# First graph's loads ahead of the constants, and adjacency loads as transfers, in the planner of a two-layer graph attention kernel

## The chip, the cores and the metric

The kernel runs on one core of a Trainium2 chip. The metric is the device time of one execution in microseconds (us); three executions of the kernel before took 3692.64 to 3694.01 us, with a median of 3692.82. The engines are named as in the profile: PE is the matrix engine, PEld its weight loads, DVE the vector engine, ACT the scalar engine, POOL GpSimd, SP the queue engine that issues most of the transfers. The profile was taken of one execution of 3692.5 us from its first to its last instruction, with a mean granted TensorE clock of 0.996.

## The reference

There are 32 graphs of 512 nodes with 512 features each, `x[32, 512, 512]` in float32, and an adjacency matrix for each, `adj[32, 512, 512]` in int32. Cut to what matters:

```
h = relu(layernorm(x))                                    # layer 0
scores = leaky_relu(h@w_src [rows] + h@w_dst [columns] + b)
attn = softmax(where(adj + I == 0, -inf, scores), rows)
x = x + attn @ h

h = relu(layernorm(x))                                    # layer 1: two attention layers
xl = h @ W1                                               # 4 heads of 256
e = leaky_relu(xl.att_src1 [sources] + xl.att_dst1 [targets])
g = softmax(where(adj > 0 or I, e, -1e9), over sources)^T @ xl + b1, heads joined
g = elu(g)                                                # 1024 features
g2 = the same with W2, att_src2, att_dst2, b2, one head of 512
x = x + g2
```

The adjacency matrix of a graph is used twice over, as a mask with the diagonal set: by rows in layer 0 and by columns in both attention layers of layer 1. Both uses need the mask and its transpose.

## The kernel before

**Work and tiles.** A graph is four tiles of 128 nodes. x of a graph is one buffer `x` (1 MB), loaded by `load_x` (L653) through SP; the adjacency matrix is loaded by `load_adj` (L660) through GpSimd, which turns int32 into bfloat16 on the way (512 KB in the buffer), once as `m0` for layer 0 (`masks0`, L673) and once as `m1` for layer 1 (`masks1`, L689). There are two places for x, one for m0, two for m1.

**A graph's path.** `layer0_scores` (L708) takes the statistics of x (L493, L494, L495 on DVE; a power of -1/2 on GpSimd, L497; L502 on DVE), makes h on ACT (L510) and two dot products of each h tile with the score vectors `ws_r` and `wd_r` on DVE (L378), adds b (L720), and makes the mask m0: four additions of the identity to diagonal blocks (L680), one pass that turns zeros into a large negative number (L683), and four transposing transfers through SP (L669). `edge_weights` (L582) makes the attention weights: row maxima on DVE (L591, then L596 and L598), spreading by PE transposes (L487), a leaky ReLU on ACT (L609), a subtraction on DVE (L612), the mask's addition on GpSimd (L614), an exponential on ACT (L617). `layer0_out` multiplies with h on PE (L627). `layer1_in` normalises again and transposes h; `layer1_project` and `layer2_project` multiply with W1 and W2 by a scheme that needs seven products instead of eight (L822), `layer1_scores` and `layer1_head` handle the four heads, `layer2_out` the last attention and the store. `masks1` makes m1 with one pass over the whole matrix (L695) and four products on the diagonal blocks (L701).

**Constants.** `load_constants` (L388) fetches the two score vectors and b of layer 0 first (with a rank 400 places ahead), then the two attention vectors of the first attention layer (into a place of the kind `E`), eight pieces of W1, and with a rank 300 places behind, b1, b2, the second attention vectors and W2. `scores_1` and `scores_2` form dot products of the weights with the attention vectors on DVE (L378 with w as input), `sums` forms the sums of weights for the seven products (L470 on DVE or L471 on GpSimd).

**What sets the order.** The kernel writes its program by a planner. Every operation is handed to `Plan.op` with the engines that can do it, a cost, what it reads and what it writes; `Plan.draft` then plays the whole program through as a list scheduler: always the engine that can begin earliest goes next, with GpSimd asked before SP when both can begin at one time, and takes the waiting operation of lowest rank among those whose inputs are there by then. The first draft's rank is the place in the program less `ahead`; each later draft, six in all, ranks by the latest time found from the draft before. The best draft gives the order in which instructions are written to each engine's queue. On the chip each engine runs its queue in that order; the waits there come from the tiles that instructions share, not from the planner's times.

A cost is (time on the engine, time to the result), and for transfers a third number: the time for which the one transfer line is taken. Such transfers queue behind each other on that line, and at most eight of them are on their way (`IN_FLIGHT`, L51). Another 60 ns (`SIGNAL`) go by before a result is seen elsewhere. `by_dma(n)` (L255) gives 350 ns of issue, 2000 ns after, and n bytes at 300 bytes per ns. A DVE pass over n elements costs n/0.96 + 70 ns and 85 more to its result; four times as fast in the mask passes. Operations with `lock=True` on DVE and GpSimd exclude each other in the draft. The calls at the start (L968 on) are `load_x(0)`, `load_constants()`, `layer0_scores(0)`, `scores_1`, `sums`, `layer0_out(0)`, `layer1_in(0)`, then `load_x(1)` and `layer0_scores(1)`, and the loop over graphs.

The places that an edit of this kind meets in the planner are these:

```
            for held in moves:
                if len(landed) >= self.IN_FLIGHT:
                    at = max(at, landed[-self.IN_FLIGHT])
                moving = max(moving, at) + held
                there += moving - at
                landed.append(at + there)
```

The other functions, with their line numbers:

## Time and profile before

| what | value |
|---|---|
| median of three executions | 3692.82 us |
| span of the profiled execution | 3692.5 us |
| transfers of the whole span | 312.17 MB, mean 85 GB/s |
| loads of adj, `m<-in_adj_dram` | 64 of 512 KB, median 7.0 us from issue to landing |
| loads of x, `x<-in_x_dram` | 32 of 1024 KB |
| transposing transfers `m0T<-m` | 128, median 4.2 us to landing |
| chain that ended last: PE, DVE, DMA | 94%, 3%, 1% of the span |

In the profile's groups a line such as "L614 POOL TENSOR_TENSOR E<-E,m" names the source line, the engine, the operation and the tiles written and read, with the digits of their names left out: m stands for m0 and m1, w for the pieces of the weights. A timeline row gives the start, the stretch, the engine, and in square brackets how long the engine had been idle before and what ended that. Engines that end in q (SPq) are the issuing of an instruction, not its work. A table of stretches gives for each the length, then busy time with the number of instructions for PE, PEld, DVE, ACT and POOL, then the granted clock of PE, the busy share of the transfer engines and the GB/s that they moved.

### The profile page before, as it was taken

The numbers are of one execution on the slowest core, as the hardware profiler recorded it, in microseconds if no ns is written. First come the engines' busy times: TensorE is split into PE (matmuls) and PEld (weight loads), VectorE is DVE, ScalarE is ACT, GpSimd is POOL, SyncE is SP. The second block draws the span as 40 slices with busy tenths as digits, with TensorE's granted clock in tenths as the row PEclk, the third lists the DMA queues.
The fourth block names the chain that finished last, engine by engine and source line by source line (L and its number), as shares of the span: only waits on it lengthen the run. The fifth ranks groups of instructions, "written<-read, shape, count | busy, mean of one in ns | idle before, by whom it ended". The sixth has DMA issues, their size and how long they took to land.

```text
span 3692.5 us, 51317 instructions
## 1 busy us (share of the span) xinstructions
PE 3625.2 (98%) x17806; PEld 3131.3 (85%) x17806; DVE 2878.2 (78%) x7478; ACT 1760.2 (48%) x3227; POOL 1592.1 (43%) x1353
## 2 busy tenths in 40 slices
PE   5899999999999999999999999999999999999998
PEld 4788888888888888888888888888888888888887
DVE  7988778877788877788877878777887778787755
ACT  2455444554454554445544445544455544455433
POOL 3534444534444444445344444444444444444332
PEclk9999999999999999999999999999999999999999
DMA  6244322334323333223333233442233422334310
GB/s 162 52 92 103 87 73 82 81 92 104 72 74 90 75 103 91 70 83 80 91 103 72 76 88 75 103 98 68 81 82 85 103 72 78 86 75 103 90 51 32
DMA packets 304342, 312.17 MB, mean 85 GB/s; under 512 B 150496, under 2 KB 188880, under 8 KB 304080
## 3 DMA queue, kind: packets, MB, share of 16 engines
q1 hardware_dynamic: 270288, 275.32, 26.2%
q0 software_dynamic: 33792, 33.56, 6.5%
q8 instruction: 140, 2.29, 0.3%
q14 instruction: 122, 1.00, 0.1%
HBM read 240.91 MB, written 67.89 MB: 84 GB/s over the span
## 4 chain that ended last, share of the span: by engine, by line
PE 94%; DVE 3%; DMA 1%; POOL 0%; issue 0%; ACT 0%; DVEq 0%; ACTq 0%
PE acc L627 46%; PE acc L822 41%; PE acc L487 4%; PE m_bank L487 2%; DVE junk L591 1%; DVE junk L378 0%; PE acc L553 0%; DVE E L612 0%; DMA m<-in_adj_dram 0%; DVE v L905 0%; POOL E_one L614 0%; DVE E_one L612 0%; DMA x<-in_x_dram 0%; DVE v L893 0%; DMA out_dram<-x 0%
## 5 line engine op out<-in xcount | busy, mean ns | idle before, releaser
L614 POOL TENSOR_TENSOR E<-E,m 128x512 f32<-128x512 f32 x512 | 620.2, 1240 | 803.3 <-DVE E L612 798.3
L627 PE MATMUL acc<-pair,E 128*128 128x257 f32 x4096 | 961.6, 381 | 1.4 <-ACT E L617 1.2
L627 PEld LDWEIGHTS acc<-pair,E 128*128 128x128 f32 x4096 | 743.0, 190 | 114.5 <-ACT E L617 14.4
L822 PE MATMUL acc<-w_T,E 128*128 128x257 f32 (+1 forms) x2048 | 521.5, 381 | 1.0 <-ACT pair L522 0.6
L627 PE MATMUL acc<-h,E_one 128*128 128x256 f32 (+1 forms) x2048 | 478.2, 382 | 6.3 <-ACT E_one L617 6.3
L617 ACT ACTIVATE E<-E 128x512 f32<-128x512 f32 x512 | 312.0, 624 | 315.4 <-POOL E L614 315.4
L627 PE MATMUL acc<-xl,E_one 128*128 128x257 f32 x1984 | 448.2, 379 | 0.0
L591 DVE CUSTOM_DVE_ANT_0 junk<-m1T,a_bank 128x512 bf16<-128x512 bf16 x640 | 436.0, 681 | 15.4 <-PE a_bank L487 1.7
L627 PEld LDWEIGHTS acc<-h,E_one 128*128 128x128 f32 x2048 | 383.8, 191 | 59.4 <-ACT E_one L617 7.6
L822 PEld LDWEIGHTS acc<-w_T,E 128*128 128x128 f32 x2048 | 379.6, 190 | 55.4 <-ACT pair L522 0.8
L627 PEld LDWEIGHTS acc<-xl,E_one 128*128 128x128 f32 x1984 | 371.4, 190 | 53.7
L612 DVE TENSOR_TENSOR E<-E,m_bank 128x512 f32<-128x512 f32 x512 | 326.5, 679 | 24.7 <-PE m_bank L487 24.7
L609 ACT ACTIVATE E<-c_row,ac 128x512 f32<-128x512 f32 x512 | 335.6, 708 | 1.9 <-DMA c_row<-lines 1.9
L520 ACT COPY pair<-acc 128x258 f32<-128x258 f32 (+1 forms) x375 | 138.2, 369 | 412.1 <-PE acc L822 410.3
L520 ACT COPY xl<-acc 128x257 f32<-128x257 f32 x219 | 81.7, 373 | 455.8 <-PE acc L822 455.8
L902 ACT ACTIVATE e<-v,minus_one 128x512 f32<-128x512 f32 x256 | 184.3, 720 | 236.4 <-DVE r L639 111.1
L645 DVE SCALAR_TENSOR_TENSOR x<-acc,r,x 128x256 f32<-128x256 f32 x512 | 240.6, 478 | 47.8 <-PE acc L627 43.6
L663 POOL DMA_DIRECT2D m<-in_adj_dram x64 | 51.4, 804 | 521.1 <-DVE col L591 476.8
L835 DVE TENSOR_TENSOR pair<-acc,pair 128x258 f32<-128x258 f32 (+1 forms) x390 | 164.5, 424 | 137.8 <-PE acc L822 127.7
L822 PE MATMUL acc<-w,hT 128*128 128x258 f32 x1024 | 268.4, 382 | 0.0
L822 PE MATMUL acc<-w,pair 128*128 128x257 f32 x1024 | 259.3, 380 | 0.0
L614 POOL TENSOR_TENSOR E_one<-E_one,m 128x512 f32<-128x512 f32 x128 | 145.0, 1165 | 263.2 <-DVE E_one L612 263.2
(108 smaller groups left out, 6117.7 us busy)
## 6 DMA issues: line engine op xcount, KB each, us to landing
a_row<-lines SPq DMA_DIRECT2D x190, 256.0 KB, 3.4
c_row<-lines SPq DMA_DIRECT2D x190, 256.0 KB, 3.5
x<-in_x_dram SPq DMA_DIRECT2D x32, 1024.0 KB
m<-in_adj_dram POOLq DMA_DIRECT2D x64, 512.0 KB, 7.0
spill<-x SPq DMA_DIRECT2D x32, 1024.0 KB, 4.3
x<-spill SPq DMA_DIRECT2D x32, 1024.0 KB
out_dram<-x SPq DMA_DIRECT2D x30, 1024.0 KB, 5.0
m0T<-m SPq DMA_TRANSPOSE x128, 4.2
```

The lines of the kernel that those rows point to most:

```text
L487: op("PE", on_pe(P, transpose=True), lambda: nc.tensor.transpose(dst_of(), src_of(), identity), src, dst(part), ahead)
L520: nc.scalar.copy(dst_of(), src_of())
L591: lambda t=t: nc.vector.tensor_tensor_reduce(junk, mask_max.at[:, t, :], a_row.at, 1.0, LOWEST, ALU.add, ALU.max, accum_out=amax.at[:, t : ...
L609: lambda t=t: nc.scalar.activation(E.at[:, t, :], c_row.at, AF.Prelu, bias=a_of(t), scale=1.0, alpha=SLOPE),
L612: op("DVE", on_dve(N), lambda t=t: nc.vector.tensor_sub(E.at[:, t, :], E.at[:, t, :], m_row.at), m_row(*ROW) + E(t), E(t))
L614: "POOL", on_pool(N, True), lambda t=t: nc.gpsimd.tensor_add(E.at[:, t, :], E.at[:, t, :], mask.at[:, t, :]),
L617: op("ACT", on_act(N), lambda t=t: nc.scalar.activation(E.at[:, t, :], E.at[:, t, :], AF.Exp), E(t), E(t))
L627: lambda s=s: nc.tensor.matmul(acc.at[:, :n], E.at[:, s, node_block(t)], of(s), start=(s == 0), stop=(s == T - 1)),
L645: lambda acc=acc, r=r, f=f, t=t: nc.vector.scalar_tensor_tensor(X.at[:, t, f], acc.at[:, :HD], r.at, X.at[:, t, f], op0=ALU.mult, op1=ALU. ...
L822: lambda k=k: nc.tensor.matmul(acc.at[:, :width], at[a]()[:, k, node_block(r)], weight_of(w, k, c), start=(first and k == 0), stop=(k == n ...
L835: op("DVE", on_dve(width), lambda: nc.vector.tensor_add(place(), acc.at[:, :width], place()), acc(0) + token, token)
L902: op("ACT", on_act(2 * F, 1), lambda e=e, ts=ts: nc.scalar.activation(e.at, v.at[:, ts, :], AF.Exp, bias=minus_one), parts, e(0))
```

## The change

At the start, two tokens are brought in that only the planner knows: `START("x")`, written by the load of x of graph 0, and `START("adj")`, written by the first load of an adjacency matrix. All other loads of x, and all constants but the two score vectors and b of layer 0, read the first; all other adjacency loads read the second. In the draft they so begin once the load they are behind has landed. The purpose is that graph 0 has the transfer line for itself at first. Besides, an adjacency load's cost changes from 2200 ns on GpSimd and 8000 to landing, outside the transfer line, to 1100 ns on GpSimd, 4500 to landing and 2800 on the line, so it also counts among the eight transfers on their way.

```
+        behind = START("x")
         att = [Buffer("E"), Buffer("E")]
         for i, vector in enumerate((att_src1, att_dst1)):
-            fetch(HF, lambda i=i: flat(att[0])[:, i * HF : (i + 1) * HF], rows(vector, HF), att[0](i), 0)
+            fetch(HF, lambda i=i: flat(att[0])[:, i * HF : (i + 1) * HF], rows(vector, HF), att[0](i), 0, behind)
...
+    START = Buffer(None)
...
     def load_x(b):
         X[b] = xb = Buffer("x")
         op(
             "SP", by_dma(4 * N * D), lambda: nc.sync.dma_start(xb.at, node_tiles(x, b)),
-            (), xb(*((t, half) for t in range(T) for half in range(2))),
+            START("x") if b else (), xb(*((t, half) for t in range(T) for half in range(2))) + ([] if b else START("x")),
         )
...
-        op("POOL", (2200.0, 8000.0), lambda: nc.gpsimd.dma_start(m.at, node_tiles(adj, b)), (), m(*ROW))
+        first = not START.wrote.get("adj")
+        op(
+            "POOL", (1100.0, 4500.0, 2800.0), lambda: nc.gpsimd.dma_start(m.at, node_tiles(adj, b)),
+            () if first else START("adj"), m(*ROW) + (START("adj") if first else []),
+        )
```

The pieces of W1, b1, b2, the second attention vectors and W2 get `behind` in the same way as the two attention vectors shown.

More of the change, by code (lines that the diff above doesn't have):

```diff
@@ L388, in load_constants, with fetch @@
     def load_constants():
-        def fetch(n, place, src, token, ahead):
-            op("SP", by_dma(4 * P * n), lambda: nc.sync.dma_start(place(), src), (), token, ahead)
+        def fetch(n, place, src, token, ahead, behind=()):
+            op("SP", by_dma(4 * P * n), lambda: nc.sync.dma_start(place(), src), behind, token, ahead)
         fetch(D, lambda: ws_r, rows(w_src, D), W["w0"](0), AHEAD)
@@ L404, in load_constants @@
                     H // 2 * F, lambda k=k, q=q: w1_s[q][:, k % (KD // 2), :, 2:], w1_k[k, :, half::2, :],
-                    W["w1"]((q, k % (KD // 2))), 0,
+                    W["w1"]((q, k % (KD // 2))), 0, behind,
                 )
-        fetch(HF, lambda: b1_r, rows(b1, HF), W["b1"](1), -LATER)
-        fetch(D, lambda: b2_r, rows(b2, D), W["b2"](0), -LATER)
+        fetch(HF, lambda: b1_r, rows(b1, HF), W["b1"](1), -LATER, behind)
+        fetch(D, lambda: b2_r, rows(b2, D), W["b2"](0), -LATER, behind)
         for i, vector in enumerate((att_src2, att_dst2)):
-            fetch(D, lambda i=i: flat(att[1])[:, i * D : (i + 1) * D], rows(vector, D), att[1](i), -LATER)
+            fetch(D, lambda i=i: flat(att[1])[:, i * D : (i + 1) * D], rows(vector, D), att[1](i), -LATER, behind)
         nk = KH // 2
@@ L416, in load_constants @@
                     nk * HD, lambda q=q, half=half: w2_s[q] if half else w2_s[q][:, :, 2:],
-                    w2_q[i, :, :, W2 - 2 :] if half else w2_q[i, :, :, : W2 - 2], W["w2"](*((q, k) for k in range(nk))), -LATER,
+                    w2_q[i, :, :, W2 - 2 :] if half else w2_q[i, :, :, : W2 - 2], W["w2"](*((q, k) for k in range(nk))), -LATER, behind,
                 )
```

## The prediction, made before the changed kernel ran

> **What bounds the kernel now.** I read the page's busy table and its 40 slices first, then busy time by stretches of 100 us and, at the start, of 10 us, then the first 30 us of the timeline, and last the landing times of the adjacency loads. Busy table and slices:

> ```profile
> PE 3625.2 (98%) x17806; PEld 3131.3 (85%) x17806; DVE 2878.2 (78%) x7478; ACT 1760.2 (48%) x3227; POOL 1592.1 (43%) x1353
> ...
> PE   5899999999999999999999999999999999999998
> ```

> The span is 3692.5 us and PE is busy for 3625.2, so all that any edit of the order can move is 67.3 us of idle PE. By stretches of 100 us, 48.4 of it lie in 0 to 100, 6.1 in 100 to 200, 2.2 in 200 to 400, none from 400 to 3600, and 10.5 after 3600. The change starts at the start, so here are stretches of it (busy us, instructions in brackets):

> ```profile
> 0.00:10.00 10.00, 0.00 (x0) 0.00 (x0) 3.00 (x11) 1.28 (x1) 3.31 (x13) 1.00 0.74 194
> 10.00:20.00 10.00, 0.00 (x0) 0.00 (x0) 1.13 (x6) 2.93 (x4) 1.22 (x1) 1.00 1.12 299
> 20.00:30.00 10.00, 2.73 (x8) 1.48 (x8) 8.73 (x23) 0.53 (x1) 0.00 (x0) 1.00 1.22 267
> 30.00:40.00 10.00, 3.71 (x10) 2.85 (x11) 9.66 (x29) 3.78 (x7) 5.61 (x5) 1.00 0.97 307
> ...
> 50.00:60.00 10.00, 3.87 (x18) 3.03 (x17) 9.41 (x34) 0.01 (x1) 3.79 (x2) 0.96 0.00 0
> ```

> The third figure is DVE. Up to 20 us nothing computes; from 22 to about 165 us DVE is full (9.3 to 10 of 10 in most stretches) and PE has holes. So DVE sets the pace of the start: a microsecond of DVE idleness before 22 us is worth about one microsecond at the end, until PE is full. The timeline of DVE there (start, duration, and in brackets idle before and what ended it):

> ```profile
> 6.08 2.47 DVE L493 BATCH_NORM_STATS2 st<-x 128x6 f32<-128x512 f32 x4 [4.49 <-DMA x<-in_x_dram]
> 8.47 0.36 DVE L494 BATCH_NORM_AGGREGATE mv<-st 128x2 f32<-128x6 f32 x4
> 14.08 0.29 DVE L680 TENSOR_TENSOR m<-m,ident 128x128 bf16<-128x128 bf16 x1 [5.24 <-DMA m<-in_adj_dram]
> 14.29 0.16 DVE L495 TENSOR_SCALAR col<-mv 128x4 f32<-128x4 f32 x1
> 14.36 0.69 DVE L680 TENSOR_TENSOR m<-m,ident 128x128 bf16<-128x128 bf16 x3
> 15.79 0.16 DVE L502 SCALAR_TENSOR_TENSOR col<-mv,col 128x4 f32<-128x4 f32 x1 [0.74 <-POOL col L497]
> 20.80 0.69 DVE L695 TENSOR_SCALAR m<-m 128x2048 bf16<-128x2048 bf16 x1 [4.84 <-DMA m<-in_adj_dram]
> 21.41 0.69 DVE L683 TENSOR_SCALAR m<-m 128x2048 bf16<-128x2048 bf16 x1
> 22.01 0.69 DVE L378 SCALAR_TENSOR_TENSOR junk<-h,ws_r 128x512 bf16<-128x512 f32 x1
> ```

> Two stalls are to be seen. L680 needs m0 of graph 0, which lands at 14.0; behind it in DVE's order stands L495, which needed only x. Then L695 needs m1 of graph 0, which is not wanted for long, and holds L683 and all eight dots for 4.84 us. The eight dots then end with L720 at 27.97.

> [...] GpSimd issues three adjacency loads at 1.51, about 2.3 and 3.27; the times to landing are 12.5, 18.3 and 21.5 us, so they land one after another, at 14.0, 20.6 and 24.8. [...]

> **The change part by part.** START is a Buffer(None): no tile. Its tokens exist for the planner only; no instruction on the chip waits for them. What the change alters is the planner's clock, and so the order on each queue. I first replayed the old rules by hand to see whether they give the traced order. Old: x lands at 2000 + 3495 = 5.5 us; m0 at 8.0, the second adjacency load at 2200 + 8000 = 10.2. Four L493 end at 7.97, L494 at 8.28, L680 is ready at 8.06, L495 only at 8.43: one L680, then L495, then three L680, as traced. L683 and L695 become ready within some 20 ns of each other at 10.25 (L680 waits out GpSimd's lock until 9.7), and L695 went first. On SP, eight transfers in flight let seven weight loads go before the mask is there, then four transposes: also as traced. So the method carries.

> New, the same way. (a) At time 0 the planner asks GpSimd before SP, so the first adjacency load takes the transfer line first: 2800, plus 4500: it lands at 7.3. x comes behind: 2800 + 3495 + 2000 = 8.3. Four L680 run from 7.36 to 8.17, L683 is ready at 8.32, x's statistics at 8.36. So the order on DVE becomes L680 x4, L683, L493 x4, L494 x4, L495, L502, dots. (b) m1 of graph 0 is now held to 7.36 and lands at 15.3, behind the dots' start; L695 falls behind the dots. (c) On SP at 8.36: x of graph 1 and the two attention vectors (three issues of 350), then at 9.4 the transposes, ready at 9.07 and more urgent; the eight W1 pieces now come after them.

> What this does on the chip: the issues ahead on both queues stay x, two score vectors, b, x of graph 1, attention vectors on SP, and three adjacency loads on GpSimd, with no wait. [...] So m0 should land at about 14.0 again, with 13 to 15 as bounds. From there, with durations of the rows above: L680 x4 and L683, 0.95 + 0.6, to 15.6; L493 x4 and L494, 2.75, to 18.35; L495, 0.15; L497 on GpSimd 1.22 (its row), to 19.8; L502 0.16; first L510 0.85, to 20.9; eight dots at 0.74, to 26.8, against 27.97. Gain 1.1. L695 (0.6) is not saved but moves behind 27 us, where DVE is full: gain left about 0.5 to 1.1. The removed stall of 4.84 is thus mostly paid back, since 2.75 of statistics that had hidden in the wait for m0 now stand behind it, and the pow, L502 and L510 lie open again.

> Transposes: SP now waits in the first of them to 15.6 instead of issuing weights; four took 6.62, to 22.2. Eight W1 pieces of 256 KB follow, 2 MB at the 267 to 307 GB/s of the stretches, 7 to 8 us: the last lands at 30 to 31. The first dot with W1 ran at 33.70, so I cost this at nothing; its cover is the work between 27 and 34 (four L591, L493 of x, L596, L598). E_one's addition ran at 35.54 behind L612, and the transposed mask is there by 25: nothing. The constants in the diff's other lines change place on SP only: nothing, since SP waits for none of them.

> (d) All 64 adjacency loads cost 1100 of issue instead of 2200 and count as transfers. In the steady part PE has no idle time, DVE is at 76 to 81%, GpSimd at 41 to 48%: nothing to win. But the whole order is drafted anew, and the holes of the start and end can fall differently. Bounds from the holes seen: PE stood 7.0 us for L510 at 60 and 5.1 at most for L598; one such hole less or more is 5 to 8 us either way. I take zero.

> Sum: 3692.8 - 1 = 3691.7.

> **Rivals.** *The loads come early.* If m0 landed as it does later (the page has 7.0 us from issue to landing), it would be there at 8.5, 5.5 us sooner, and the chain above ends at 21.3: 6.6 us sooner; were x's statistics also first, the dots would end near 17.5, 10.5 us sooner. Some 9 us: 3683.5. For it: the purpose of the edit, and 299 GB/s in 10 to 20 us, so the line is crowded. Against it: nothing on the chip holds the other loads back. *The new order opens a hole* (slower). Statistics behind m0 make DVE depend on the slowest load; should m0 land at 15 to 16, the gain of 1.1 is a loss of about 1, and W1 arriving with the dots, with one more hole of the 7 to 8 us kind, gives +8 to +10: 3702. For it: W1's margin is only 3 us. Against it: DVE had work up to 33.7 for which W1 isn't needed. *A steady-state stall* of 0.3 us per graph over 30 graphs would also give about 9 us; against it speaks the 100% of PE at only 78% of DVE.

> **How the numbers follow.** Stalls trade places, 0.38; early loads, 0.35; a new hole, in either place, 0.27. The bound of 0.2% is 7.4 us. Of the first case I give 0.15 to faster and 0.1 to slower by redrafting, of the second 0.8 to faster, of the third 0.9 to slower: faster 0.34, same 0.38, slower 0.28. The range reaches to both other cases with a little of their spread: 3679 to 3705.

> **What would show it.** Right: DVE starts with L680 at about 14.0, L683 ahead of L493, no L695 before the dots, L720 at about 27; on SP the transposes ahead of W1; PE full from 400 to 3600. Wrong: L493 at 6 with dots from 11 to 15 us (early loads); m0 landing at 8 to 10; DVE waiting for W1 after 28; or idle PE in the steady stretches.

## The result, and the profile after

The changed kernel is slower: 3712.12 us (median of four executions, 3707.61 to 3713.91) against 3692.73, a ratio of 1.0051 with a 95% interval of 1.0033 to 1.0068. The forecast was 3691.7 with a range of 3679 to 3705. The execution that was profiled took 3707.61 us, so the trace shows the smallest loss of the four; the kernel before was profiled in an execution of 3694.24 us. The two traces therefore differ by 13.1 us where the medians differ by 19.4. The changed kernel's busy table and its PE slices:

```profile
span 3705.6 us, 51345 instructions
...
PE 3629.8 (98%) x17806; PEld 3139.6 (85%) x17806; DVE 2814.7 (76%) x7349; ACT 1810.4 (49%) x3355; POOL 1589.4 (43%) x1354
...
PE   5899999999999999999999999999999999999998
```

PE runs the same 17806 instructions. Its idle time has grown from 67.3 to 75.8 us, and its busy time by 4.6 us. The slices don't say where. For that I compared, from the two traces, the time at which the k-th PE instruction ended (lag of the changed kernel, us):

```
k            100   300   400   500   600  1500  5500  9500  13500  17500  17806
before, us    67   122   147   169   189   375  1184  1995   2806   3617   3689
lag, us     +2.4  +4.4  +8.8  +8.0  +8.7  +6.6  +7.4  +9.3  +11.0  +13.3  +13.1
```

So there are two losses: one of 8.7 us in the first 190 us, of which 6.6 are left at 375 us, and a slow drift of 6.7 us from 375 to 3617 us, where the kernel before had a full PE.

**The first graph.** This is the timeline of DVE in the changed kernel, from its first wait:

```profile
13.69 0.90 DVE L688 TENSOR_TENSOR m<-m,ident 128x128 bf16<-128x128 bf16 x4 [12.09 <-DMA m<-in_adj_dram]
14.62 0.69 DVE L691 TENSOR_SCALAR m<-m 128x2048 bf16<-128x2048 bf16 x1
15.23 2.46 DVE L495 BATCH_NORM_STATS2 st<-x 128x6 f32<-128x512 f32 x4
...
20.38 0.69 DVE L378 SCALAR_TENSOR_TENSOR junk<-h,ws_r 128x512 bf16<-128x512 f32 x1 [0.88 <-ACT h L512]
...
26.35 0.23 DVE L728 TENSOR_SCALAR ac<-ac,b_r 128x4 f32<-128x4 f32 x1
26.48 0.69 DVE L703 TENSOR_SCALAR m<-m 128x2048 bf16<-128x2048 bf16 x1
```

L688 and L691 are the old L680 and L683, L703 is the old L695, L728 the old L720. The mask stands ahead of the statistics, m1's pass behind the dots, and the dots end at 26.4 instead of 28.0. PE's first product follows at 35.79 instead of 37.41. The gain is then lost. In the stretches (third figure DVE, then ACT and GpSimd, then PE's granted clock), DVE falls from 9.79 to 6.78 us busy in 40 to 50, and PE has deeper holes than before at 60 to 70 (6.95 against 9.11) and 100 to 110 (6.22 against 10). The kernel before, then the changed one:

```profile
40.00:50.00 10.00, 10.00 (x42) 8.55 (x42) 9.79 (x28) 0.63 (x1) 3.61 (x3) 1.00 0.57 113
60.00:70.00 10.00, 9.11 (x38) 7.94 (x39) 9.32 (x11) 8.70 (x16) 9.65 (x6) 0.70 0.01 2
100.00:110.00 10.00, 10.00 (x39) 8.39 (x39) 9.50 (x27) 4.86 (x8) 7.51 (x5) 0.82 0.53 91
```

```profile
40.00:50.00 10.00, 10.00 (x45) 8.61 (x44) 6.78 (x29) 0.00 (x0) 0.80 (x2) 1.00 0.36 54
60.00:70.00 10.00, 6.95 (x27) 6.00 (x28) 8.85 (x20) 6.84 (x12) 8.68 (x5) 0.56 0.01 2
100.00:110.00 10.00, 6.22 (x17) 4.79 (x18) 9.68 (x31) 4.01 (x8) 5.67 (x5) 0.52 0.65 93
```

In PE's timeline two holes have grown. The first stands in front of the transposes of h, the second in front of a spreading of m (before, then changed):

```profile
60.86 3.67 PE L487 MATMUL acc<-ident,h 128*128 128x128 f32 x16 [6.99 <-ACT h L510]
95.74 1.11 PE L487 MATMUL m_bank<-ident,col 128*128 128x128 f32 x4 [5.14 <-DVE col L598]
```

```profile
63.02 3.68 PE L489 MATMUL acc<-ident,h 128*128 128x128 f32 x16 [10.35 <-ACT h L512]
101.25 1.11 PE L489 MATMUL m_bank<-ident,col 128*128 128x128 f32 x4 [7.95 <-DVE col L600]
```

**The steady part.** Who waited for whom, DVE from 400 to 3500 us: total, times and longest. The kernel before, then the changed one:

```profile
DVE m L695 <- DMA m<-in_adj_dram: 2.0, 4, 1.0
```

```profile
DVE m L703 <- DMA m<-in_adj_dram: 35.5, 17, 3.5
DVE m L688 <- DMA m<-in_adj_dram: 2.0, 3, 0.9
```

and PE's waits of the changed kernel in the same stretch, of which the kernel before has none:

```profile
PE m_bank L489 <- DVE col L600: 3.2, 6, 0.8
```

These 3.2 us are less than the drift. The records of PE's products overlap (one of L629 is recorded as 0.38 us long, and the next starts 0.22 us after it), so a short wait can be hidden in them; their starts tell more. From the 1500th to the 17500th PE instruction, the time from one start to the next sometimes exceeds the median of its kind by more than 60 ns. Summed up, this excess is 8.7 us in the changed kernel and 1.5 before. In front of L489, waiting for L600, stand 4.9 of it, and nearly all the rest in front of L629, mostly in pieces of about 0.1 us.

One of the six waits, in the chain that ended last:

```profile
1233.66 8.79 DMA m<-in_adj_dram
...
1242.56 0.70 DVE m L703
...
1247.50 0.08 DVE col L600
1247.58 0.04 issue
1247.62 0.65 PE m_bank L489 x4
```

The load of a later graph's m1 takes 8.79 us. DVE waits for it in L703, though this mask is not urgent: its transposes (L677) are issued only from 1338.8 us on. Behind L703 in DVE's queue stand the row maxima (L593, L600) that PE is about to need. In the kernel before, the median time from the issue of the m1 load to L695 is 8.2 us, and DVE waited in four graphs, where it took 8.6 to 9.3. In the changed kernel DVE is free for the pass 5.9 us after the issue (median), and the load isn't there yet. The loads themselves land in 5.4 to 9.2 us before (median 6.9) and in 5.4 to 9.3 after (median 7.7): somewhat later in the middle, hardly later at the top. So the pass has moved earlier, and the loads a little later. The reason for the first, which e1, e4 and e6 test, should be the draft: it now expects a load after 4500 + 2800 = 7.3 us, where it had been told 8.0.

### The profile page after: what moved, and what is told of

Read it like the earlier page. It is cut to its first block, busy times and chain, and to the rows that moved or that the text cites. A ratio compares the mean times of both kernels' runs of the same rounds, so it can differ in the third digit from the quotient of the medians.

```text
span 3705.6 us, 51345 instructions
## 1 busy us (share of the span) xinstructions
PE 3629.8 (98%) x17806; PEld 3139.6 (85%) x17806; DVE 2814.7 (76%) x7349; ACT 1810.4 (49%) x3355; POOL 1589.4 (43%) x1354
## 2 busy tenths in 40 slices
PE   5899999999999999999999999999999999999998
## 4 chain that ended last, share of the span: by engine, by line
PE 91%; DVE 4%; DMA 2%; POOL 1%; ACT 1%; issue 0%; SPq 0%; DVEq 0%; POOLq 0%; ACTq 0%
PE acc L629 45%; PE acc L830 39%; PE acc L489 4%; PE m_bank L489 2%; DMA m<-in_adj_dram 2%; DVE junk L593 1%; POOL E_one L616 1%; DVE junk L378 0%; PE acc L555 0%; DVE E L614 0%; DVE v L913 0%; ACT E L611 0%; DVE E_one L614 0%; ACT E L619 0%; DVE v L901 0%
## 5 line engine op out<-in xcount | busy, mean ns | idle before, releaser
L629 PE MATMUL acc<-pair,E 128*128 128x257 f32 x4096 | 962.1, 382 | 0.6 <-ACT E L619 0.5
L629 PEld LDWEIGHTS acc<-pair,E 128*128 128x128 f32 x4096 | 751.2, 190 | 108.4 <-ACT E L619 8.4
L629 PE MATMUL acc<-h,E_one 128*128 128x256 f32 (+1 forms) x2048 | 489.1, 382 | 5.3 <-ACT E_one L619 5.3
L593 DVE CUSTOM_DVE_ANT_0 junk<-m1T,a_bank 128x512 bf16<-128x512 bf16 x640 | 436.5, 682 | 32.3 <-ACT a_bank L581 16.4
L629 PE MATMUL acc<-xl,E_one 128*128 128x257 f32 x1984 | 448.5, 379 | 0.0
L629 PEld LDWEIGHTS acc<-h,E_one 128*128 128x128 f32 x2048 | 385.5, 191 | 59.7 <-ACT E_one L619 6.2
L629 PEld LDWEIGHTS acc<-xl,E_one 128*128 128x128 f32 x1984 | 370.6, 189 | 54.4
L522 ACT COPY pair<-acc 128x258 f32<-128x258 f32 (+1 forms) x428 | 157.7, 369 | 353.0 <-PE acc L830 350.4
L830 PE MATMUL acc<-w,E 128*128 128x257 f32 (+1 forms) x1024 | 261.6, 380 | 0.0
L830 PE MATMUL acc<-w,pair 128*128 128x257 f32 x1024 | 250.8, 379 | 0.4 <-ACT pair L524 0.4
```

Source lines behind the costliest of these rows:

```text
L522: nc.scalar.copy(dst_of(), src_of())
L593: lambda t=t: nc.vector.tensor_tensor_reduce(junk, mask_max.at[:, t, :], a_row.at, 1.0, LOWEST, ALU.add, ALU.max, accum_out=amax.at[:, t : ...
L629: lambda s=s: nc.tensor.matmul(acc.at[:, :n], E.at[:, s, node_block(t)], of(s), start=(s == 0), stop=(s == T - 1)),
L830: lambda k=k: nc.tensor.matmul(acc.at[:, :width], at[a]()[:, k, node_block(r)], weight_of(w, k, c), start=(first and k == 0), stop=(k == n ...
```

## The experiments

All were timed in five rounds beside the kernel before. "Lag" is the lag of the 600th PE instruction (189 us in the kernel before); "drift" is the lag of the 17500th less that of the 1500th; "waits" are DVE's waits for loads of adj from 400 to 3500 us. These three are from the profiled execution, which lay up to 4.8 us from its kernel's median (e6; e7's was the slowest of 21, 2.7 above). So a lag or a drift is good to some 3 us: e8, e11 and e13 drift by -2.1 to -2.9 though the kernel before had no idle PE there that could be saved.

```
kernel                        median us  ratio (95% interval)       lag   drift  waits
changed                        3712.12   1.0051 (1.0033 to 1.0068)  +8.7   +6.7  37.5
e1  new cost alone             3711.73   1.0053 (1.0039 to 1.0066)  +2.2  +15.0  45.6
e2  tokens alone               3700.12   1.0020 (1.0012 to 1.0027)  +5.9    0.0   1.4
e3  before, SIGNAL 61          3691.45   0.9998 (0.9990 to 1.0006)  -2.9   +0.2   none
e4  changed, landing 9.3       3695.33   1.0006 (0.9998 to 1.0014)  -0.7   +2.3   none
e5  changed, constants free    3708.16   1.0043 (1.0029 to 1.0057)  +2.6  +13.1  47.0
e6  before, landing 7.3        3766.82   1.0203 (1.0189 to 1.0217)  +9.0  +68.2  82.0
e7  before, line, 8.0          3698.39   1.0015 (1.0008 to 1.0021)  -1.7   +8.4  10.1
e8  tokens, landing 10         3684.52   0.9977 (0.9968 to 0.9987)  -3.0   -2.7   none
e9  changed, SIGNAL 61         3710.95   1.0048 (1.0036 to 1.0061)  +6.2  +11.8  42.6
e10 changed, SIGNAL 58         3711.78   1.0051 (1.0039 to 1.0064)  +7.3  +12.2  70.7
e11 e8, SIGNAL 58              3686.92   0.9984 (0.9978 to 0.9991)  -2.3   -2.1   none
e12 before, landing 10         3685.43   0.9980 (0.9972 to 0.9988)  -6.3   -0.9   none
e13 e8, constants free         3692.89   1.0000 (0.9992 to 1.0009)  +5.9   -2.9   none
e14 e5, SIGNAL 58              3714.40   1.0062 (1.0048 to 1.0076) +10.9  +10.3  72.7
e15 token on W1 only           3705.89   1.0033 (1.0021 to 1.0046)  +3.5   +9.3  42.3
```

**e1 and e2: each half of the change by itself.** e1 is the kernel before with

```
-        op("POOL", (2200.0, 8000.0), lambda: ...
+        op("POOL", (1100.0, 4500.0, 2800.0), lambda: ...
```

> The kernel before with the new cost of the adjacency loads (1100, 4500, 2800) and no START tokens. Landing theory (the planned time from issue to landing went from 8.0 to 7.3 us, the chip needs up to 9, so the m1 mask pass stands too early in DVE's queue): DVE waits for m1's load in most graphs of the steady part, some 20 to 40 us in all against 2.0 before, and PE ends the steady part 4 to 8 us late. Start theory (the adjacency load takes the planner's line before x, statistics of x behind the mask, W1's dots late): present here too, since the planner's order at time 0 comes from the cost alone: +5 to +9 us by 200 us. So 3703 to 3712. Redrafting theory (any change of the draft scatters by several us, no particular cause): anywhere from 3685 to 3710, with no more DVE waits for m1 than before.

e2 is the changed kernel with `(2200.0, 8000.0)` back.

> The changed kernel with the old cost of the adjacency loads (2200, 8000, not on the line), START tokens kept. Landing theory: the steady part is as before (DVE waits for m1's load about 2 us in all). Start theory: x's statistics run at 6 us again, m1's mask pass is behind the dots, so the dots end at about 23 instead of 28 us; PE is not late at 200 us, perhaps 2 to 5 us early. So 3687 to 3693. Redrafting theory: no forecast of a sign, 3685 to 3710.

The drift goes with the cost: +15.0 us with the cost alone, none with the tokens alone. At the start it is the other way from what the start theory said: e1 has the same order of DVE as the changed kernel up to its dots (mask, then statistics, dots to 25.8), yet lags by only 2.2. So putting the mask ahead of the statistics isn't what loses 8.7 us. And e2, from which no loss was expected, is 5.9 late at 189 us and loses over 7 us in all, without drift: the tokens with the old cost make the start late in this draft, and what in them does it isn't shown.

The starts of PE's instructions show that e1's drift is of the changed kernel's kind: an excess of 16.2 us against 1.5 before, 12.3 of it in front of L487, waiting for L598.

**e3: a redraft without a reason.** `SIGNAL = 61.0` in the kernel before.

> The kernel before with the planner's SIGNAL at 61 instead of 60 ns: nothing that means anything on the chip, but the program is drafted anew. This measures what a redraft by itself does. Landing and start theory: within 4 us of before (3689 to 3697), no more DVE waits for m1's load, since the planned landing stays 8.0 us. Redrafting theory: 8 us or more away from before, either way.

No steady drift and no waits, and the same time within the interval. The start moved for nothing, by 2.9 us at 189 us and by 5.9 at 375: differences of this size between two starts can't be argued about here.

**e4: a later landing in the changed kernel.** `(1100.0, 6500.0, 2800.0)`, so 9.3 us with the line free.

> The changed kernel with 6500 instead of 4500 ns from issue to landing of an adjacency load, so 9.3 us with the line free, all else as changed. Landing theory: DVE's waits for m1's load in the steady part fall from 35.5 us to under 5, and the drift of 5 to 6 us between 400 and 3600 us is gone; the loss of the start stays. So 3699 to 3703 if the start stays at +8. Start theory alone: the same as the changed kernel, 3707 to 3713. Redrafting theory: no forecast.

The waits are gone, and 16.8 of the 19.4 us with them. The drift fell to 2.3 us, which DVE's waits for adj don't explain any more: the starts of PE's instructions put 5.7 us in front of L629, all in pieces of about 0.1 us, and none in front of L489. The start came along too: from +8.7 to -0.7, which was not expected, so the time lies below the forecast.

**e5: constants without the token**, `behind = ()` in the changed kernel.

> The changed kernel without the token on the constants (W1, W2, attention vectors, biases are drafted as in the kernel before); the tokens between x and x, adj and adj and the new cost stay. Start theory (W1 comes late in the draft, so its dots stand behind the reciprocal L641, which waits for PE): the 3.0 us wait of DVE for L641 is gone and PE's lag at 200 us falls from 8.7 to 0 to 3 us. Landing theory: waits of DVE for m1's load in the steady part stay at 30 to 45 us, drift 4 to 15 us. So 3699 to 3710. If the start is only a matter of how the draft falls, the lag at 200 us is anything between -4 and +9.

The lag fell as the start theory said, but its mechanism didn't show: DVE still stood 2.0 us for the reciprocal L641. Drift and waits stayed.

**e6 and e7: which part of the cost.** e6 is the kernel before with `(2200.0, 7300.0)`; e7 with `(1100.0, 5200.0, 2800.0)`.

> The kernel before with one number changed: an adjacency load lands 7300 instead of 8000 ns after its start in the draft; issue of 2200, no line, no tokens. Landing theory: this alone brings the waits of DVE for m1's load in the steady part (20 to 45 us against 2.0) and a drift of 4 to 15 us between 375 and 3617 us. If it is the counting on the line and in flight that spoils the steady part, waits stay near 2 us and the drift is 0. The start is left open (-4 to +9). So 3692 to 3715 by the first, 3688 to 3701 by the second.

> The kernel before with adjacency loads of 1100 ns issue, counted on the line (2800), and 5200 after, so that with the line free they land at 8.0 us as before; no tokens. Landing theory: waits of DVE for m1's load in the steady part under 10 us, drift 0 to 3 us. If the counting on the line or the shorter issue spoils the steady part: waits of 20 us or more, drift 4 or more. Start: adjacency first on the line, as in the changed kernel, lag -4 to +4 at 200 us. So 3689 to 3699 by the first.

e6 changes one number by 0.7 us, and the kernel loses 74 us. DVE's and PE's waits from 400 to 3500 us:

```profile
DVE m L680 <- DMA m<-in_adj_dram: 44.3, 27, 3.1
DVE m L695 <- DMA m<-in_adj_dram: 37.7, 25, 2.8
```

```profile
PE m_bank L487 <- DVE col L598: 43.8, 34, 2.9
PE acc L822 <- ACT pair L520: 2.0, 3, 1.1
```

Here both masks are taken too early in nearly every graph, and PE pays for it 34 times. The drift is 68.2 us where 4 to 15 were forecast, and the time far above its range; the mechanism is the one that was named. By the starts of PE's instructions, 50 us of the drift stand in front of L487. In e7, with 8.0 us again but on the line, m1's pass no longer waits; there are 10.1 us of waits of m0's L680 and 5.0 us for loads of x, and a drift of 8.4 where 0 to 3 was expected. So 8.0 us on the line aren't the same as 8.0 us off it. e7 also takes the shorter issue (1100 for 2200 ns), and its trace is of its slowest execution; which of the two changes costs this I didn't separate. The steady loss of the changed kernel needs neither: e6 has it with the old issue and off the line, and e4 is rid of most of it with both in place.

**e8: a landing above the 9.3 us that the two kernels show at most**, `(1100.0, 10000.0)` in the changed kernel, off the line.

> The changed kernel with adjacency loads at 1100 ns of issue, off the line, landing after 10000 ns; tokens kept. Landing theory: a landing above the longest that the chip shows (9.3 us) leaves no wait for m1's load in the steady part and no drift. Start: x's statistics ahead of the mask, m1's pass behind the dots. So 3684 to 3692, faster than both kernels if the start isn't late. If a redraft scatters the start, up to 3697.

It is faster than both kernels, by 8 us against the one before. DVE has no waits for adj, and the first graph goes as the purpose of the change wanted:

```profile
6.28 2.47 DVE L495 BATCH_NORM_STATS2 st<-x 128x6 f32<-128x512 f32 x4 [4.68 <-DMA x<-in_x_dram]
13.41 0.90 DVE L688 TENSOR_TENSOR m<-m,ident 128x128 bf16<-128x128 bf16 x4 [2.85 <-DMA m<-in_adj_dram]
14.84 0.69 DVE L691 TENSOR_SCALAR m<-m 128x2048 bf16<-128x2048 bf16 x1
20.59 0.22 DVE L728 TENSOR_SCALAR ac<-ac,b_r 128x4 f32<-128x4 f32 x1
```

The statistics run while the mask is still coming, the layer normalisation is through before it lands, and the dots end at 20.6 us, 7.4 earlier than in the kernel before. The adjacency load itself came no sooner than 13.4 us, although the next two now left GpSimd's queue at 10.3 and 11.1 us instead of 2.5 and 3.3.

**e9 to e12: is it the draft or the change?** e9 and e10 are the changed kernel with SIGNAL at 61 and 58, e11 is e8 with 58, e12 is the kernel before with `(2200.0, 10000.0)`.

> The changed kernel with the planner's SIGNAL at 61 instead of 60 ns: a redraft with nothing else changed. Landing theory: the steady part keeps its waits of DVE for m1's load (30 to 45 us) and a drift of 4 to 15 us, because the planned landing is still 7.3 us. Draft theory of the start (the 8.7 us at 200 us are how this draft happened to fall): the lag at 200 us differs from 8.7 by 4 us or more. Cause theory of the start (tokens and the new cost make it late in any draft): the lag stays at 7 to 10. So 3700 to 3708 by the first, 3707 to 3716 by the second.

> The changed kernel with SIGNAL at 58 ns, a second redraft of it. Same forecasts as for 61: steady waits 30 to 45 us and a drift of 4 to 15 us in any case; lag at 200 us within 7 to 10 if the change itself makes the start late, scattered if it is the fall of the draft.

> The version with tokens and a landing of 10000 ns off the line, redrafted with SIGNAL at 58. Landing theory: no waits for m1's load in the steady part, no drift above 1 us. Draft theory of the start: lag at 200 us between -6 and +4. So 3682 to 3695; if the gain of this version is robust, 3683 to 3688.

> The kernel before with one number changed: an adjacency load lands 10000 instead of 8000 ns after its start in the draft; no tokens, issue 2200, off the line. Landing theory: steady part without waits for m1's load, a drift of -3 to 0 us (the 2.0 us of waits before cost PE nothing). If the tokens are what gains at the start in the version with 10000, this one is 3 to 7 us slower than it: 3687 to 3692; if it is the later landing that puts m1's pass behind the dots, it is as fast: 3683 to 3687.

The changed kernel's loss isn't an unlucky draft: all three drafts of it are within 1.2 us of each other in time, with a lag of 6.2 to 8.7 and waits of 37.5 to 70.7. Their profiled executions took nearer their medians than the first one's, and show a drift of about 12 us: with a lag of about 7 this makes up the 19 us. The two grown holes of the first graph are in them as well: 10.3 and 10.7 us in front of the transposes of h, 7.9 and 7.8 in front of the spreading of m. e11 and e12 keep most of e8's gain. As e12 has no tokens and is as fast as e8 within the spread of both, the tokens add nothing that was seen at a landing of 10.0. e6, the kernel before and e12 differ in one number only, a planned landing of 7.3, 8.0 and 10.0 us: DVE's waits for adj are 82.0, 2.0 and none, and the times 3766.82, 3692.7 and 3685.43 us. In e12, too, the dots end early, without any token:

```profile
6.19 2.47 DVE L493 BATCH_NORM_STATS2 st<-x 128x6 f32<-128x512 f32 x4 [4.60 <-DMA x<-in_x_dram]
8.98 0.17 DVE L495 TENSOR_SCALAR col<-mv 128x4 f32<-128x4 f32 x1
12.58 0.90 DVE L680 TENSOR_TENSOR m<-m,ident 128x128 bf16<-128x128 bf16 x4 [2.10 <-DMA m<-in_adj_dram]
14.00 0.69 DVE L683 TENSOR_SCALAR m<-m 128x2048 bf16<-128x2048 bf16 x1
19.76 0.22 DVE L720 TENSOR_SCALAR ac<-ac,b_r 128x4 f32<-128x4 f32 x1
```

**e13 to e15: does the token on the constants cost the start?** Up to here a version with that token was some 3 to 6 us later at 189 us than a like one without it (e8 and e12, the changed kernel and e5, e2 and the kernel before). e13 takes it from e8, e14 is e5 redrafted with 58, and e15 keeps it only on W1 and the first attention vectors (the line of W2 is shown; b1, b2 and the second attention vectors lose it in the same way):

```
-                    nk * HD, ..., W["w2"](*((q, k) for k in range(nk))), -LATER, behind,
+                    nk * HD, ..., W["w2"](*((q, k) for k in range(nk))), -LATER,
```

> The version with tokens and 10000 ns, but without the token on the constants. If that token costs 3 to 6 us at the start in any draft: lag at 189 us of -6 to -8 against -3.0 and -2.3 with it, and 3679 to 3684. If the differences are the fall of the draft: lag anywhere from -6 to 0 and no faster than 3684. No steady drift over 3 us either way, by the landing theory.

> The changed kernel without the token on the constants, redrafted with SIGNAL at 58. If the token costs 3 to 6 us in any draft: lag at 189 us of 0 to 4, against 6.2, 7.3 and 8.7 in the three drafts with it. If it is the fall of the draft: outside that. Landing theory: waits for m1's load 30 to 70 us, drift 6 to 13.

> The changed kernel with the constants' token left on the first attention vectors and W1 only; W2, b1, b2 and the second attention vectors are free of it. If the token's cost comes from W1 (its dots planned late): lag at 189 us 6 to 9, as in the changed kernel. If it comes from W2 and the rest: lag 0 to 4. Landing theory: drift 6 to 13.

That theory falls. Without the token e8 got 8.9 us later at 189 us, and e5's redraft lags by 10.9, more than any draft with it. The pairs before had been the fall of the drafts; so is e15's lag of 3.5, which alone would have spoken for a cost of the token on W2. In e13 the dots end at 21.1 us, 6.9 earlier than in the kernel before, and PE is still 5.9 late at 189 us. The steady part did in all three what the landing theory said: no waits and no loss in e13, waits and drifts of 10.3 and 9.3 in the other two.

## Why the prediction was wrong, point by point

**What the order at the start would be: right.** Replaying the planner's rules by hand gave the mask ahead of the statistics, m1's pass behind the dots and the transposes ahead of W1 on SP; all three are in the trace. So are the times: L680's counterpart began at 13.69 (forecast 14.0), the dots ended at 26.35 (26.8). The point that nothing on the chip holds the other loads back also held: GpSimd issued the next two adjacency loads at 2.5 and 3.3 us, and that of graph 0 landed at 13.7, not at 8.5, so the second case, early loads, did not come. The three landings that the prediction gives, at 14.0, 20.6 and 24.8 us, show the order of GpSimd's own loads and nothing of how SP's fell among them.

**What followed from it: wrong.** The sum kept 0.5 to 1.1 us of that gain. What failed is the price: "a microsecond of DVE idleness before 22 us is worth about one microsecond at the end", with W1's later place costed "at nothing" and the redraft at "zero". The dots did end 1.6 us earlier, and the 600th product came 8.7 us later. The price fails in other versions too: in e4, e8, e12 and e13 the dots end 5.6, 7.4, 8.2 and 6.9 us earlier, and the lag is -0.7, -3.0, -6.3 and +5.9.

Between the first product (1.6 us early) and 67 us the changed kernel lost 4.0 us; DVE was busy for 34.6 us from 30 to 70 where it had been busy for 38.2, and 3.0 of that is one wait:

```profile
44.06 0.17 DVE L641 RECIPROCAL r<-acc 128x1 f32<-128x1 f32 x1 [3.02 <-PE acc L629]
```

DVE waited for a product while W1's dots stood behind it, and PE's hole in front of the transposes of h grew by 3.4 us. W1's bytes were not late, since no dot waited for them; its dots were placed late, the first at 36.14 instead of 33.70. But e8, e11 and e12 have the same wait (3.2 to 3.3 us) and are early, so it is part of this draft's loss and not the cause that sets the versions apart. The rest, 6.4 us by 147 us, came as holes of PE, up to 7.95 us long in front of the spreading of m, with DVE busy on dots of the weights (L378), and as slow products behind the holes (0.43 us from start to start, where others took 0.22). The two grown holes recur in all three drafts of the changed kernel, so they are no accident of one draft, but no cause of the start's loss has been shown. What stays open: with a planned landing of 7.3 us all eight drafts lag at 189 us (2.2 to 10.9 us); of the other nine, the kernel before among them, two lag (5.9 both) and six lead. That points to the landing here too, but a start moves by several us with a redraft, and no run shows how the landing would do it.

**The steady part: wrong, and here the cause is shown.** The step that failed is (d). It read "In the steady part PE has no idle time, DVE is at 76 to 81%, GpSimd at 41 to 48%: nothing to win", and took zero. It looked for a gain in the new cost and only asked what could be won; that the planned landing had moved from 8.0 to 7.3 us, close to the median of 7.0 for all loads and below the longer ones (up to 9.2 in the trace before), stood in its own numbers and was not followed up. The rival named a "steady-state stall of 0.3 us per graph" and set against it that PE was at 100% with DVE at 78%. That was no argument: in the chain above DVE, 76% busy on the average, stood idle for 1.36 us until L703's load was there, with L593 and L600 behind it in its queue. e1 brings the stall in by the cost alone and e6 by the landing alone; e4 takes most of it out by a longer landing alone, and e8, which also leaves the line, the rest. Measured, the term taken as zero is a drift of 12 us in e9 and e10, some 0.4 us for each graph, and 10.0 us of it in both stand in front of PE's L489, waiting for DVE's L600.

**The range.** It let one hole or one stall come, 8 to 10 us, as one case of 0.27. Both came together, some 7 and some 12 us, and the range had not added them.

## What to carry to other kernels

Where a planner writes in-order queues, a planned transfer time that is too short is far dearer than one that is too long: too short, and an operation that nobody needs yet stands at the head of a queue and holds what is urgent (0.7 us too few in one number cost 74 us in e6; in the changed kernel the same landing of 7.3 us came with some 12 us of drift); too long, and the operation comes a little later than it could, which cost nothing seen here at 10.0 us, the longest that was tried. Set such times above the upper end of the landing times in the trace, not at the median. And judge a new ordering by several drafts that differ in nothing that matters: with nothing changed but a signal's planned time by 1 or 2 ns, the lag moved by 0.7 to 2.9 us here, and once by 8 (e5 to e14).

## What the runs showed of the hardware

Slow products stood behind holes of PE. Up to 200 us the records of the granted clock put PE at half its clock for 20.5 us before and for 34.1 us in the changed kernel; it was busy for 13.7 and 18.4 us of that. Products of 128x257 started 0.43 us apart where the records show half the clock and 0.22 where they show the full one. (The records begin at 41 to 42 us. The products just before that started 0.43 us apart too, though the stretches show a clock of 1.00 there.) So about 2.4 us of the start's loss, by estimate half of the 4.7 between 13.7 and 18.4, are slow products. Two such stretches of the changed kernel, and the hole ahead of the second (the one ahead of the first is that of 10.35 us):

```profile
55.10:68.70 13.60, 5.65 (x21) 4.87 (x22) 12.45 (x28) 5.54 (x9) 8.85 (x6) 0.50 0.00 1
133.60:137.00 3.40, 3.40 (x10) 2.71 (x9) 3.37 (x12) 3.19 (x6) 0.00 (x0) 0.50 0.02 5
```

```profile
133.11 0.69 PE L489 MATMUL m_bank<-ident,col 128*128 128x128 f32 x4 [2.65 <-DVE col L600]
```

The landing times of one kind of load spread widely in the steady part. From 400 to 3500 us the same 512 KB of adjacency took from 5.3 us (e9) to 10.2 (e1) in ten of the traces (the kernel before, the changed one, e1, e3, e4, e6 to e9 and e12), with medians of 6.9 (the kernel before) to 8.2 us (e6) that differ from draft to draft. The first load of all, issued at 1.5 us, took 12.5 us in the kernel before and 12.2 in the changed one; the addition on DVE that waited for it (L680, L688) began at 12.6 (e12) to 14.1 us (the kernel before) in twelve traces (these two, e1 to e5, e8 to e12).
